# Moving block loads ahead of a write on one DMA queue, and reading partial sums with one DMA instead of four

## The chip, the cores and the metric

The kernel runs on one core of one Trainium2 chip. A core has five engines with an instruction stream each: TensorE (PE), which multiplies matrices and loads their stationary operand (PEld), VectorE (DVE), ScalarE (ACT), GpSimd (POOL) and SyncE (SP), which here only issues DMAs. They synchronise by semaphores. Data move between DRAM and the on-chip memory by 16 DMA engines. The metric is the device time of one execution in microseconds (us); lower is better.

## The reference, cut to what matters

The input is 128 graphs of 128 nodes with 512 features each, and a 0/1 adjacency matrix for each graph. Two layers follow, each with a residual and a layer norm: a graph attention with 8 heads of 64 units, and a hypergraph convolution with a hidden width of 1024.

```python
def _L0_gnn_ref(X, A, W, b, a_self, a_neigh):
    feats = jnp.einsum('bnf,hfu->bhnu', X, W)
    e_self = jnp.einsum('bhnu,hu->bhn', feats, a_self)
    e_neigh = jnp.einsum('bhnu,hu->bhn', feats, a_neigh)
    dense = e_self[..., :, None] + e_neigh[..., None, :]
    dense = jax.nn.leaky_relu(dense, negative_slope=0.2)
    dense = dense + NEG_BIG * (1.0 - A[:, None, :, :])
    att = jax.nn.softmax(dense, axis=-1)
    out = jnp.einsum('bhij,bhju->bhiu', att, feats) + b[None, :, None, :]
    ...
    return jax.nn.relu(out)

def hypergraph_conv(x, adj, W, b):
    H = (adj != 0).astype(x.dtype)
    w = adj.reshape(N, -1)[:, :C]
    xw = jnp.einsum('ncd,hd->nch', x, W)
    Dn = jnp.einsum('nce,ne->nc', H, w)
    Dn = jnp.where(Dn > 0, 1.0 / Dn, 0.0)
    Be = H.sum(axis=1)
    Be = jnp.where(Be > 0, 1.0 / Be, 0.0)
    m = Be[:, :, None] * jnp.einsum('nce,nch->neh', H, xw)
    out = Dn[:, :, None] * jnp.einsum('nce,neh->nch', H, m)
    return out + b
...
h = jax.nn.relu(hypergraph_conv(x, adj, W1, b1))
h = layer_norm(h, gamma, beta)
y = hypergraph_conv(h, adj, W2, b2)
return y + x
...
x = _layernorm(x + _L0_gnn_ref(x, adj, ...), axis=-1)
x = _layernorm(x + _L1_gnn_ref(x, adj, ...), axis=-1)
```

The layer norm of the hidden `h` needs the mean of the squares of `h` over 1024 features for each node.

## The kernel before, in words

The graphs are worked on in 64 pairs. A software pipeline runs over the pairs: in each period of about 36 us one pair is in each of several stages, so that a pair passes from its first load to its store within about five periods. The order of the instructions is written out by hand. Every step has a lag (in periods) and a time (in us, within a nominal period `T = 38.6`); the list `todo` holds all steps of all pairs with the time `(p + lag) * T + time`, is sorted by it, and the instructions are issued in that order. These times are only an order: on the chip each engine goes through its own instructions in this order and waits on semaphores where data or a buffer aren't there yet.

In the text a period begins with the first matmul of `propagate` (output `pz`) of a pair, and a place in it is given in us from there.

The stages that the change and the prediction touch:

- **Loads of a pair.** `load` brings the adjacency (`a`) and its first row, spread over the partitions (`w`); it stands at the very start of the period on SP's queue. `load_blocks` (lines 122 to 129) brings x once more in blocks of 32 nodes, as four DMAs of 128 KB in rows of 512 B, into `xb`. `load_edges` (lines 131 to 137) brings the adjacency in blocks, four DMAs of 32 KB in rows of 128 B, into `ab`. Both tiles have one buffer. They are read by `x_transpose` (line 384, two instructions on DVE, the second at place 35.0 of the written order) and `edges` (line 420, at 35.75), which turn the blocks in place of a transpose on TensorE.
- **Attention scores.** `spread_rows` (line 541) transposes the two score columns of the new features into `rows` on DVE and writes them to DRAM as `rd` (line 551, 16 KB). `neighbours` (line 569) reads `rd` back, spread over all partitions, into `nb`, one DMA of 512 KB for each of the two graphs. POOL adds the mask (line 588), ACT takes the leaky ReLU (line 604), DVE the maximum (line 610) and ACT the exponential (line 618), by half graphs.
- **Turning the exponentials.** `e_write` (line 622) writes the exponentials of a graph to DRAM (`ed`, 512 KB), `e_read` (line 630) reads them back with four DMAs in another order (`eb`), and `e_transpose` (line 639) finishes the transpose on DVE into `eT`. TensorE then multiplies them with the features (`pav`, line 702). SP's queue holds, in this order: `ed` of graph 0, its four `eb`, `ed` of graph 1, its four `eb`. Each `eb` waits on SP until its `ed` has landed, and what stands behind it waits too.
- **Sums of squares.** ACT squares `h` (line 891), POOL adds the squares down to one block of 128 (line 903). `sum_blocks` (lines 949 to 954) transposes and reduces on DVE, `write_sums` (line 959) writes 16 KB to DRAM (`sd`), `read_sums` (line 965) reads 8 rows of 32 numbers with each of four DMAs into `sums_out`, and `sum_rest` (lines 973 and 975) transposes this 128x32 tile on DVE and adds eight numbers for each of the two graphs. The result, after POOL's power (line 1002), scales the output (line 1006).
- **Hidden layer.** `propagate` (line 815, `pz`), its eviction `zT` on ACT (line 828), POOL's sums `zS` (line 839), then the products `ph`, whose matmuls all stand in the helper at line 97. TensorE runs the hidden products, the features (`pf`), the attention (`pav`) and the output products (`py`, `pq`) one after another in a fixed order.

On SP's queue a period so holds: the four reads of sums, `a` and two `w`, `ed` and four `eb`, `ed` and four `eb`, a small write `dd_d` (line 373), four `xb`, the store of a finished pair (line 1041), four `ab`, `rd`, two `nb`, a read `dnb` (line 575), `sd`, and the rows of x for the residual (line 120).

The places of the two block loads in the written order:

```python
for p in range(PAIRS):
    if p > 1:
        todo.append(({2: 79.5, 3: 143.1}.get(p, p * T), load, (p,)))
        todo.append((16.2 if p == 2 else p * T + 19.0, load_blocks, (p,)))
        todo.append((p * T + (28.5 if p == 2 else 20.5), load_edges, (p,)))
```

Of the kernel before, what the change touches and what calls it, by code (L numbers as in the profile page):

```python
# [8 lines left out]
F32 = mybir.dt.float32  # L9
AF = mybir.ActivationFunctionType  # L10
ALU = mybir.AluOpType
AX = mybir.AxisListType
# [8 lines left out]
def kernel(  # L21
# [45 lines left out]
    nc = tc.nc  # L67
    G, N, F = x.shape
    P = 128
# [10 lines left out]
    B = 32  # L80
    NB = P // B

    const = ctx.enter_context(tc.tile_pool(name="const", bufs=1))
    work = ctx.enter_context(tc.tile_pool(name="work", bufs=1))
# [126 lines left out]
    for i in range(2):  # L211
        t = const.tile([P, 2, H, UW + 1], F32, name=f"ft{i}")
# [1 line left out]
        fts.append(t)  # L214
    dn = const.tile([P, B], F32, name="dn")
    nc.gpsimd.memset(dn, 0.0)
    sums_in, sums_out = (const.tile([P, B], F32, name=n) for n in ("sums_in", "sums_out"))
    for t in (sums_in, sums_out):
        nc.gpsimd.memset(t, 0.0)

# [94 lines left out]
    def step(lag, time, since=0, until=PAIRS):  # L315

        def keep(fn):
            steps.append((lag, time, fn.__name__, range(since, until), fn, ()))
            return fn
        return keep  # L320
# [640 lines left out]
    @step(3, 31.5, until=LAST - 1)  # L961
    def read_sums(p, s):

        for c in range(NB):
            nc.sync.dma_start(
                sums_out[c * B:c * B + 2 * NB],
                s["sd"][:, 2 * c:2 * c + 2, :].rearrange("b g n -> b (g n)"),
            )

    @step(4, 1.7, until=LAST - 1)  # L970
    def sum_rest(p, s):
        t = work.tile([P, B], F32, tag="so", name=f"so_{p}")
        nc.vector.transpose(t, sums_out)
        s["ve"] = small.tile([P, 2], F32, tag="ve", name=f"veh_{p}")
        nc.vector.tensor_reduce(
            s["ve"], t[:, :2 * NB].rearrange("p (b g) -> p g b", g=2), AX.X, ALU.add
        )

    @step(3, 43.0, since=LAST - 1, until=LAST)
# [142 lines left out]
    for t, fn, *args in (  # L1122
# [14 lines left out]
    T = 38.6  # L1137
    todo = [
        (11.1, prepare_first, (0,)), (12.0, prepare_first, (1,)), (15.45, prepare_first_sums, ()),
        (12.1, load_weights, (nc.scalar, w2_blocks, w2t, DH // 2, QU)),  # L1140
        (13.05, prepare_vectors, ()),
        (14.05, load_weights, (nc.scalar, w1_blocks[:2], w1t, F // 2, HALF)),
        (12.95, load_first_row, (1,)),
        (15.46, load_weights, (nc.sync, w1_blocks[:1:-1], w1t, F // 2, HALF)),
        (16.1, everywhere, (b2_bc, b2, nc.sync)),
        (79.0, prepare_hidden, (nc.gpsimd, 0)), (79.1, prepare_hidden, (nc.gpsimd, 1)),
# [55 lines left out]
    for p in range(PAIRS):  # L1202
        if p > 1:
            todo.append(({2: 79.5, 3: 143.1}.get(p, p * T), load, (p,)))
            todo.append((16.2 if p == 2 else p * T + 19.0, load_blocks, (p,)))
            todo.append((p * T + (28.5 if p == 2 else 20.5), load_edges, (p,)))
        for lag, time, name, pairs, fn, args in steps:
            if p not in pairs:
                continue
            if p == 0 and lag == 2 and time < 8.5:  # L1210
                time *= 0.2
            if p == LAST:

                time = {
                    ("attend", 0): 24.25, ("attended", 0): 25.5,
                    ("attend", 1): 25.95, ("attended", 1): 26.0,
                    ("residual", 1): 26.3, ("rstds", "a"): 26.4,
                }.get((name,) + args[:1], time)
            if p == LAST - 1:
                time = {  # L1220
                    ("product", 2): 24.22 if (lag, time) > (3, 20.0) else time,
                    ("product", 5): 29.5 if (lag, time) > (3, 20.0) else time,
                    ("squares", 0): 26.5, ("squares", 1): 26.6, ("h_sums", 2): 22.3,
                    ("h_rstd",): 4.6, ("y_scale", 1): 5.8, ("y_scale", 0): 5.9,
                }.get((name,) + args[:1], time)
            time += (p + lag) * T
            todo.append((
                first.get((name, p) + args, first.get((name, p), time)), run, (fn, p, args)
            ))
# [46 lines left out]
```

## Time and profile before

| | |
|---|---|
| time, median of 3 runs | 2395.53 us (2391.52 to 2398.6) |
| the profiled execution | 2395.0 us |
| its span, first to last instruction | 2393.2 us |
| granted TensorE clock, mean | 0.998 of full speed |
| DVE idle before line 973, waiting for `sums_out` | 49.0 us in 36 of 62 times |
| POOL idle before line 588, waiting for `nb` | 30.4 us in 25 times, the longest 5.1 us |
| SP's wait for `ed` to land, before `eb` (line 630) | 375.8 us in 126 times, the longest 5.2 us |
| SP's wait for `sd` to land, before the reads of sums (line 965) | 125.0 us in 62 times |

The profile is that of one execution. Its times belong to that execution and are set against its own 2395.0 us, which lies 1.8 us above its span. "Busy" of an engine is time in an instruction; matmuls are pipelined and their ends are modelled, so a busy TensorE isn't one at its peak. The chain of waits is followed back from the last instruction to what released it at each step. Idle time of an engine that isn't the one others wait for costs nothing. DMA issues on SP show the time that SP takes to issue, not the transfer; the trace also has records of the single packets of the DMA engines, with their start, length and queue, but not which of the 16 engines ran them.

### The profile page before, as it was taken

To read this page: it belongs to the slowest core of one execution; us is meant where nothing else is said; L and a number is where in the kernel's file an instruction comes from. 1 tells how busy PE (TensorE), PEld (TensorE's weight loads), DVE (VectorE), ACT (ScalarE), POOL (GpSimd) and SP (SyncE) were. 2 spreads that over 40 slices of the span, in tenths; PEclk is the share of its full clock that TensorE was granted. 3 is DMA by queue.
4 is the path that set the end of the run, shared out by engine and by line. 5 is a ranking of instruction groups with operands and counts; after the bars stand their busy time and mean duration, and the time that the engine had idled before them with its cause. 6 is when DMAs were issued, how large, how long until landed. Compare 5 with 4: busy or idle time off the path is not lost.

```text
span 2393.2 us, 81039 instructions
## 1 busy us (share of the span) xinstructions
PE 2359.4 (99%) x32309; PEld 1986.4 (83%) x32309; DVE 2079.3 (87%) x4456; ACT 1529.5 (64%) x4481; POOL 1827.5 (76%) x2060
## 2 busy tenths in 40 slices
PE   7999999999999999999999999999999999999998
PEld 6788888888888888888888888888888888888886
DVE  7988888888898898888888888988988988988875
ACT  4565765756667667667667666676676676676663
POOL 5877787777777877877877778778778778777774
PEclk9999999999999999999999999999999999999999
DMA  6545555555455455454554554545554555545541
GB/s 197 133 142 155 142 142 143 146 149 150 139 156 143 144 156 147 140 152 149 146 150 147 149 150 143 156 146 139 155 148 143 153 146 141 151 147 151 148 130 37
DMA packets 432874, 347.12 MB, mean 145 GB/s; under 512 B 153177, under 2 KB 382065, under 8 KB 432497
## 3 DMA queue, kind: packets, MB, share of 16 engines
q1 hardware_dynamic: 429024, 337.46, 49.2%
q8 instruction: 256, 4.19, 0.7%
q10 hardware_dynamic: 3472, 4.47, 0.6%
q14 instruction: 122, 0.99, 0.2%
HBM read 239.08 MB, written 102.73 MB: 143 GB/s over the span
## 4 chain that ended last, share of the span: by engine, by line
PE 81%; DMA 7%; DVE 5%; ACT 2%; POOL 2%; SPq 2%; issue 1%; DVEq 0%; POOLq 0%; ACTq 0%
PE phX L97 16%; PE pyX L97 15%; PE pfX L97 8%; PE phW L97 8%; PE pyW L97 7%; PE phY L97 4%; PE pq L97 4%; PE pfW L97 4%; PE pav L702 4%; PE pz L97 4%; PE pyY L97 4%; DMA nb<-rd 3%; PE pfY L97 2%; DMA rd<-rows 1%; DMA ed<-nb 1%; ACT nb L604 1%
## 5 line engine op out<-in xcount | busy, mean ns | idle before, releaser
L343 ACT COPY py<-pyX 128x257 f32<-128x257 f32 x189 | 70.8, 374 | 533.8 <-PE pyX L97 458.4
L97 PEld LDWEIGHTS phX<-zS,w_sb 128*64 128x64 f32 x6144 | 348.8, 137 | 37.9 <-POOL ft L741 22.3
L97 PE MATMUL phX<-zS,w_sb 128*64 128x128 f32 x6144 | 371.9, 273 | 3.2 <-ACT ph L343 2.9
L903 POOL TENSOR_TENSOR sq<-sq 128x512 f32<-128x512 f32 (+2 forms) x384 | 344.7, 898 | 20.1
L588 POOL TENSOR_TENSOR nb<-nb,neg 128x512 f32<-128x512 f32 x256 | 320.2, 1286 | 31.1 <-DMA nb<-rd 30.4
L604 ACT ACTIVATE nb<-nb,ft 128x128 f32<-128x128 f32 x1020 | 325.1, 392 | 19.4 <-POOL nb L588 19.4
L618 ACT ACTIVATE nb<-nb,nm 128x128 f32<-128x128 f32 x1024 | 319.5, 392 | 5.1 <-DVE nm L610 4.9
L766 POOL TENSOR_TENSOR rso<-veo,mhalf 128x2 f32<-128x2 f32 x63 | 44.2, 702 | 337.6 <-DVE veo L764 337.6
L97 PE MATMUL pyX<-w_sb,h 128*64 128x257 f32 x2016 | 242.8, 379 | 0.5 <-ACT py L343 0.5
L97 PE MATMUL pyX<-w_sb,hS 128*64 128x257 f32 x2016 | 243.1, 379 | 0.0
L97 PE MATMUL pyW<-w_sb,hS 128*64 128x256 f32 x2016 | 242.5, 378 | 0.0
L880 ACT ACTIVATE h<-h,vecs 128x128 f32<-128x128 f32 x768 | 239.9, 394 | 2.5 <-DVE h L865 1.4
L610 DVE TENSOR_REDUCE nm<-nb 128x4 f32<-128x512 f32 x256 | 175.3, 685 | 48.1 <-ACT nb L604 42.7
L97 PEld LDWEIGHTS pyX<-w_sb,h 128*64 128x64 f32 x2016 | 166.4, 136 | 53.5 <-ACT py L343 0.9
L97 PEld LDWEIGHTS pyW<-w_sb,hS 128*64 128x64 f32 x2016 | 168.1, 136 | 50.1 <-issue 0.3
L741 POOL TENSOR_TENSOR ft<-ft,b_bc 128x512 f32<-128x512 f32 x128 | 202.9, 1605 | 6.2 <-ACT ft L532 6.2
L97 PEld LDWEIGHTS pyX<-w_sb,hS 128*64 128x64 f32 x2016 | 161.9, 136 | 43.8
L639 DVE STREAM_TRANSPOSE eT<-eb 128x512 f32<-128x512 f32 x252 | 163.5, 685 | 1.3 <-issue 0.4
L804 DVE SCALAR_TENSOR_TENSOR o<-y,b_bc 128x512 f32<-128x512 f32 x128 | 164.0, 1320 | 0.0
L1006 DVE SCALAR_TENSOR_TENSOR y<-y,rsh,bw_bc 128x512 f32<-128x512 f32 x126 | 150.1, 1229 | 15.2 <-POOL rsh L1002 15.2
L891 ACT ACTIVATE sq<-h 128x512 f32<-128x512 f32 x256 | 160.9, 630 | 2.1
L468 POOL TENSOR_TENSOR hS<-h 128x512 f32<-128x512 f32 x126 | 162.1, 1286 | 0.0
(178 smaller groups left out, 5630.3 us busy)
## 6 DMA issues: line engine op xcount, KB each, us to landing
nb<-rd SPq DMA_DIRECT2D x127, 512.0 KB
ed<-nb SPq DMA_DIRECT2D x126, 512.0 KB
eb<-ed SPq DMA_DIRECT2D x504, 128.0 KB
x<-in_x_dram SPq DMA_DIRECT2D x64, 512.0 KB
out_dram<-o SPq DMA_DIRECT2D x63, 512.0 KB
xb<-in_x_dram SPq DMA_DIRECT2D x248, 128.0 KB
a<-in_adj_dram SPq DMA_DIRECT2D x64, 128.0 KB
w<-in_adj_dram SPq DMA_DIRECT2D x128, 64.0 KB
```

What stands on the lines that cost most here:

```text
L97: nc.tensor.matmul(to[rows], lhs[:, rows], rhs, start=start, stop=stop, skip_group_check=True)
L468: engine.tensor_tensor(t[:, i], in0, in1, op=op)
L588: nc.gpsimd.tensor_tensor(t, t, neg[:, :, None, :].to_broadcast([P, NB, HH, B]), op=ALU.add)
L604: nc.scalar.activation(t, t, AF.Prelu, bias=s["ft"][:, g, h, 0:1], alpha=SLOPE)
L610: nc.vector.tensor_reduce(s["nm"][:, g, hs], scores(p, s, g, hs).rearrange("p b h j -> p h b j"), AX.XY, ALU.max, negate=True,)
L618: nc.scalar.activation(t, t, AF.Exp, bias=s["nm"][:, g, h:h + 1])
L639: nc.vector.transpose(s["eT"][:, g, hs, :].rearrange("p h (b i) -> p h b i", b=NB), s["eb", g][:, :, hs, :].rearrange("p b h j -> p h b j"),)
L741: nc.gpsimd.tensor_tensor(t, t, b0_bc.rearrange("p (h u) -> p h u", h=H), op=ALU.add)
L804: nc.vector.scalar_tensor_tensor(s["o"][:, g, :], s["y"][:, g, :], 2.0, b2_bc, op0=ALU.mult, op1=ALU.add)
L880: nc.scalar.activation(dst[:, k, :], src[:, k, :], AF.Relu, bias=b1_sb[:, c:c + 1])
L891: nc.scalar.activation(s["sq"][:, g, q * KH // 2:(q + 1) * KH // 2, :], hid(s, g, q), AF.Square, scale=DH ** -0.5,)
L903: nc.gpsimd.tensor_tensor(t[:, :n, :], t[:, :n, :], t[:, n:2 * n, :], op=ALU.add)
```

## The change

Two things are changed.

For the pairs from the fifth on (`p` of 4 and more), `load_blocks` moves from 19.0 to 2.0 and `load_edges` from 20.5 to 3.0 in the pair's first period. On SP's queue the eight DMAs so stand behind the loads of `a` and `w` of the same pair and ahead of the first `ed` write of the pair two places before, where they stood behind the second graph's `eb` reads and `dd_d`, the `ab` loads also behind the store. The pairs 2 and 3 keep their places. The order on the other engines stays as it was.

`read_sums` becomes one DMA for four: it reads the whole 4x8x32 numbers as 16 pieces of 64 numbers into partitions 0, 32, 64 and 96 of a `sums_out` that is now 128x256. `sum_rest` transposes all of it (128x256 in place of 128x32), into a work tile of the same size, and adds the first column of each 32x32 block. `sums_out` is set to zero once at the start, as before.

```diff
-    sums_in, sums_out = (const.tile([P, B], F32, name=n) for n in ("sums_in", "sums_out"))
+    sums_in = const.tile([P, B], F32, name="sums_in")
+    sums_out = const.tile([P, NB, 2 * B], F32, name="sums_out")
     for t in (sums_in, sums_out):
         nc.gpsimd.memset(t, 0.0)
...
     @step(3, 31.5, until=LAST - 1)
     def read_sums(p, s):
 
-        for c in range(NB):
-            nc.sync.dma_start(
-                sums_out[c * B:c * B + 2 * NB],
-                s["sd"][:, 2 * c:2 * c + 2, :].rearrange("b g n -> b (g n)"),
-            )
+        nc.sync.dma_start(
+            sums_out[::B],
+            s["sd"][:, :2 * NB, :].rearrange("b (c g) n -> c b (g n)", c=NB),
+        )
 
     @step(4, 1.7, until=LAST - 1)
     def sum_rest(p, s):
-        t = work.tile([P, B], F32, tag="so", name=f"so_{p}")
-        nc.vector.transpose(t, sums_out)
+        t = work.tile([P, NB, 2, B], F32, tag="so", name=f"so_{p}")
+        nc.vector.transpose(t.rearrange("p b g n -> p (b g n)"), sums_out.rearrange("p b x -> p (b x)"))
         s["ve"] = small.tile([P, 2], F32, tag="ve", name=f"veh_{p}")
         nc.vector.tensor_reduce(
-            s["ve"], t[:, :2 * NB].rearrange("p (b g) -> p g b", g=2), AX.X, ALU.add
+            s["ve"], t[:, :, :, 0].rearrange("p b g -> p g b"), AX.X, ALU.add
         )
...
-            todo.append((16.2 if p == 2 else p * T + 19.0, load_blocks, (p,)))
-            todo.append((p * T + (28.5 if p == 2 else 20.5), load_edges, (p,)))
+            todo.append((16.2 if p == 2 else p * T + (19.0 if p == 3 else 2.0), load_blocks, (p,)))
+            todo.append((p * T + {2: 28.5, 3: 20.5}.get(p, 3.0), load_edges, (p,)))
```

## The prediction

> **What bounds the kernel now.** I read the page's busy shares first, then busy time by stretches, the chain of waits, and the issues on SyncE's queue (SP).
>
> ```profile
> PE 2359.4 (99%) x32309; PEld 1986.4 (83%) x32309; DVE 2079.3 (87%) x4456; ACT 1529.5 (64%) x4481; POOL 1827.5 (76%) x2060
> ...
> q8 instruction: 256, 4.19, 0.7%
> ```
>
> TensorE (PE) is busy for 99% of the span, so the question is where its few idle microseconds lie. Two stretches, cut where a period begins (at the first matmul of `propagate`), with the busy time of each engine:
>
> ```profile
> 127.60:645.78 518.18, 512.60 (x7058) 430.10 (x7056) 449.54 (x965) 334.93 (x985) 399.44 (x450) 1.00 0.51 146
> 645.78:2246.14 1600.36, 1600.36 (x22179) 1356.64 (x22177) 1414.90 (x3039) 1048.49 (x3081) 1250.22 (x1409) 1.00 0.52 148
> ```
>
> The second is 44 periods of 36.37 us with PE busy throughout: nothing off PE can shorten them, only lengthen them. The first is 14 periods of 37.01 us on average, an excess of 518.18 - 14 x 36.37 = 9.0 us. That is nearly all the change can win. What it consists of, in the chain that ended last (start, duration):
>
> ```profile
> 596.32 3.42 DMA rd<-rows
> ...
> 599.76 7.18 DMA nb<-rd
> ...
> 611.55 1.97 PE phX L97 x32
> ```
>
> The small write of the neighbour scores to DRAM (`rd`, 16 KB) lands 3.42 us after its issue, only then is the broadcast read `nb` issued, POOL's masking waits 3.0 us for it, then leaky, the eviction of pz, and PE. SP's wait for that landing in the two stretches (total, times, longest):
>
> ```profile
> SPq L569 <- DMA rd<-rows: 35.3, 14, 3.1
> ...
> SPq L569 <- DMA rd<-rows: 48.8, 44, 2.1
> ```
>
> 2.5 us each against 1.1. SP's issues in a period without a stall (start, duration, number):
>
> ```profile
> 645.58 1.88 SPq L965 DMA_DIRECT2D sums_out<-sd  x3
> ...
> 652.40 0.33 SPq L622 DMA_DIRECT2D ed<-nb  x1
> ...
> 663.16 3.18 SPq L129 DMA_DIRECT2D xb<-in_x_dram  x4
> 667.86 0.41 SPq L1041 DMA_DIRECT2D out_dram<-o  x1
> 668.31 2.42 SPq L137 DMA_DIRECT2D ab<-in_adj_dram  x4
> 670.91 0.34 SPq L551 DMA_DIRECT2D rd<-rows  x1
> ```
>
> Here `rd` goes when its data are ready (670.88); in stalled periods the `ab` issues end up to 0.4 us after that. The packet records show what happens then. Of `rd`'s 128 packets 120 run 0.84 to 1.1 us after its issue, stalled or not. In the stalled periods the last eight, one DMA engine's share, come 2.0 to 2.6 us after it, when a 16,384-byte packet of the instruction queue has ended. Such a packet began 0.56 to 0.86 us after the issue of `rd` in six late cases, 1.28 to 1.42 in five, 1.31 in the period before them. From 1.41 on `rd` mostly won, between 1.23 and 1.4 either. So `rd` races an instruction refill; from the page one takes 0.007 x 16 x 2393.2 / 256 = 1.05 us.
>
> **What the Trainium skill says.** "DMA: Bandwidth & Descriptors", Queues, rings and completion order: each DMA engine takes descriptors in ring order and turns between the queue rows it has work for. The eight late packets agree. "Runtime: NRT & Kernel Launch", Instruction fetch mechanics: instructions are refilled in 16 KiB blocks, a cost called mostly hidden. The size agrees (4.19 MB / 256); hidden it is not where `rd` waits. "Perfetto Trace Analysis", DMA Instruction, HWDGE: the profiled window is descriptor generation, not data. This agrees (0.34 us for `rd`, 3.42 to its landing), so issues are priced twice below, on SP and in the rings. "VectorE: DVE Perf Modes", The three transpose paths: 32x32 blocks are transposed each by itself, so one filled row per block becomes the one filled column that `sum_rest` then reads; no run so far shows that layout.
>
> **The change, part by part.** The sum starts from the profiled execution: 2395.0 us, of which 2393.2 are the span; the runs' median, 2395.53, lies 0.5 above.
>
> *Loads moved up.* Per pair from the fifth on, eight issues (four `xb`, 1.9 us; four `ab`, 2.4) pass `ed` and `eb` of both graphs and `dd_d` on SP; `ab` passes the store too. POOL's and the other engines' queues keep their order. The loads wait for the second transpose of x and the edge transpose of the pair before, which end 1.3 us before a period begins: no block for SP.
> (a) `rd` goes at once when `rows` are done and finds the rings emptier. Its first packets came 0.84 us after issue where `ab` had ended early and 0.9 to 0.95 where just before, so it gains 0.1 us there and 0 to 0.4 us on SP. The 9.0 us by the `rd` before each stall: four late ones with the refill at 1.3 to 1.42, or SP late by 0.4 us, cost 3.35; now clear of it, I take 2.9 back. Two (1.28, 1.37), with little gain on SP, cost 2.5: even chances and a smaller loss, 1.6 back. Six (0.56 to 0.86) still meet the refill and cost 3.2: their `nb` goes 0.1 to 0.4 us sooner, and as loss grew from 0.1 to 1 us over a delay of half a microsecond, 1.4 back. Together -5.9; bounds 0 and -9.0. Late next is PE itself.
> (b) In the period at 2246.14 SP reached `rd` 1.35 us late and the next lasts 36.76, 0.39 too much: -0.3, bounds 0 and -0.4.
> (c) The first `ed` write is what gets delayed. Where sums are read early (the period shown), the new order reaches it at 644.9 + 0.65 + 0.5 + 1.0 + 1.9 + 2.4 = 651.4, before its exponentials end at 652.3: no delay. Where late (0.92 us into the period at 1154.92), at 7.4 us instead of 6.6: 0.8 us. In the rings `xb` and `ab` are 1,024 x 27 ns / 16 + 1,024 x 12 ns / 16 = 2.5 us of work, of which I guess up to 1.5 still ahead of `ed`. Behind `ed` on SP stand its `eb` read, the second `ed` and its `eb`, so they move by 0 to 2.3 us. The last `eb` landed 18.3 to 20.5 us into the period where the records tell it; VectorE (DVE), busy without a gap from 9.4 us on, takes it (`eT`) at 22.65 and comes no earlier, and PE needs the result 0.2 to 0.35 us after it is done. Cover 2.2 to 4.3 us: cost 0; if it's gone, each us beyond costs a us in each of 59 periods.
> (d) Start: in the period at 87.39 SP stands until 9.2 us for DVE's `dr`; then 4.3 us of loads put the first `ed` at 13.9 instead of 10.0. Part is made up, as `ed` then took 4.9 us to land; I put the last `eb` at 26.6 to 27.6 against `eT` at 26.6: +0.4, bounds 0 and +1.
>
> *One read for four.* Three issues of 0.60 us and their gaps leave SP in each period: 1.9 us, which pays for much of (c). The new DMA, 16 pieces of 256 B, isn't in the trace; I take 0.65 us of issue and a landing like that of the first of the four, bounds 0.5 and 1.2 on SP. DVE's transpose grows from 128x32 to 128x256, which two rows price:
>
> ```profile
> L949 DVE STREAM_TRANSPOSE sq<-sq 128x256 f32<-128x256 f32 x62 | 27.1, 437 | 0.0
> ...
> L973 DVE STREAM_TRANSPOSE so<-sums_out 128x32 f32<-128x32 f32 x62 | 13.0, 209 | 49.4 <-DMA sums_out<-sd 49.0
> ```
>
> 437 - 209 = 0.23 us, x62 = 14 us, ahead of DVE's own waits for ACT and POOL (1.47, 0.21 and 0.22 us in the period at 645.78), and 49.0 us of waiting for `sums_out` shrink: 0, bounds 0 and +14. The reduction's strided reads, 0 to 0.1 us each, have the same cover; the larger memset stands before POOL's 3.46 us wait for the first weights.
>
> Sum: 2395.0 - 5.9 - 0.3 + 0.4 = 2389.2 us.
>
> **Rivals.** *No change (0.18).* `rd` keeps meeting refills, as both keep their places. For it: six of twelve late cases, and one with `rd` on time (25.13 us in the period at 571.19). Against it: the others were late on SP. It gives 2392 to 2396, say 2394 us.
> *All stalls gone (0.14).* Without the first late ones the lag never starts: 2395.0 - 9.0 - 0.4 = 2385.6 us. Against it: the six early refills.
> *Slower (0.18).* Behind the block loads and a refill (one begins about 9 us into a period), the last `eb` lands after DVE comes for it, and PE waits before the attention matmuls. For it: the loads fill most DMA engines just then. Against it: (c), and stalled periods that issued that `eb` 3 us later without a wait there. It decides from 2.2 to 4.3 us of delay; 0.4 us beyond, 59 x 0.4 = 24 us: 2413 us.
>
> **How the numbers follow.** The forecast has 0.50, its own range 2387 to 2392. Within 0.3% (about what a measurement of this kernel can tell from no change) is 2388.3 to 2402.7. Faster: all of the second rival and 0.24 of the forecast's 0.50, as half its range lies at that bound: 0.38. Same: 0.26 + 0.18 = 0.44. Slower 0.18. The range 2385.0 to 2397.0 leaves out the last case.
>
> **What would show it.** Right: fewer periods over 36.37 us after 127.6, each behind an `rd` that met a refill; `rd` issued within 0.05 us of `rows`; the wait for `sums_out` smaller, `so` at 0.44 us; the first `ed` 0 to 1 us later. Wrong: waits of `pav` for `eT` or of `eT` for `eb` in steady periods; early excess near 9 us, or none.

## The result and the profile after

| | before | after |
|---|---|---|
| time, median of 6 runs each on one chip | 2394.76 us | 2414.18 us (2406.28 to 2414.9) |
| ratio of the runs, with 95% interval | | 1.0076 [1.006, 1.0092] |
| the profiled execution, its span | 2395.0, 2393.2 us | 2406.28, 2404.5 us |

The change makes the kernel slower, by 0.76%. (A ratio here is taken over all runs, not from the medians.) The profiled execution is the quickest of the six runs of after; it carries 11.3 us of the loss. No trace shows where the other 8 us of a usual run lie.

The first line of the page of after, and busy time by stretches of after, cut at the same matmuls as before; the last two rows are 34 and 10 periods (stretch, its length, then busy time of PE, PEld, DVE, ACT and POOL):

```profile
PE 2360.5 (98%) x32309; PEld 2009.4 (84%) x32309; DVE 2083.8 (87%) x4456; ACT 1527.8 (64%) x4481; POOL 1822.8 (76%) x2060
```

```profile
128.73:649.32 520.59, 512.30 (x7058) 435.23 (x7056) 447.21 (x965) 333.13 (x982) 396.47 (x449) 1.00 0.52 145
649.32:1886.21 1236.89, 1236.89 (x17139) 1059.47 (x17136) 1099.43 (x2348) 810.30 (x2382) 966.02 (x1090) 1.00 0.53 148
1886.21:2256.76 370.55, 364.56 (x5042) 312.80 (x5040) 322.21 (x690) 237.72 (x701) 282.69 (x320) 1.00 0.53 145
```

PE's own work is what it was. In the middle stretch it is still back to back, 36.38 us for each period. The loss lies around it. The 14 early periods are 2.4 us longer than before (520.59 against 518.18), although the `rd` stalls should have gone. The ten late ones are 370.55 - 10 x 36.37 = 6.9 us too long, where before their excess was 0.3 us. What lies ahead of the early ones took 1.1 us more; the middle and the end make up the remaining 1.2 us of the 11.3.

The waits of PE, of DVE and of SP in after (who waits, for what: total, times, longest; most lines of after stand one further down than in before):

```profile
PE pav L703 <- DVE eT L640: 13.4, 9, 2.3
```

```profile
DVE eT L640 <- DMA eb<-ed: 17.4, 12, 2.4
```

```profile
SPq L631 <- DMA ed<-nb: 402.3, 126, 5.7
...
SPq L137 <- DMA w<-in_adj_dram: 52.0, 60, 1.6
...
SPq L623 <- DMA xb<-in_x_dram: 23.1, 27, 1.8
```

The attention matmuls wait for the transposed exponentials, these for the last `eb`, and this is what the prediction named as the sign of being wrong. The wait for `sums_out` (49.0 us before) is down to 0.8 us, as forecast. New on SP are two waits that I hadn't priced: 60 times, in 48 periods, the last issues of `ab` stand still until a load of `w` has landed, and in 27 periods the first `ed` (line 623) until an `xb` has. In the periods looked at, the DMA waited for is the one eight places before on SP's queue: the fourth `ab` waits for the second `w`, and `ed` for the first `xb`.

The second worst of the late periods begins at 2182.15. SP's issues in it (start, length, number), and then the chain that ends at its late attention matmul (start, duration):

```profile
2183.56 0.94 SPq L112 DMA_DIRECT2D w<-in_adj_dram  x2
2184.60 2.37 SPq L129 DMA_DIRECT2D xb<-in_x_dram  x4
2187.07 2.88 SPq L137 DMA_DIRECT2D ab<-in_adj_dram  x4
2191.56 0.34 SPq L623 DMA_DIRECT2D ed<-nb  x1
2196.17 1.73 SPq L631 DMA_DIRECT2D eb<-ed  x4
```

```profile
2184.60 6.89 DMA xb<-in_x_dram
...
2191.56 4.59 DMA ed<-nb
...
2198.01 3.48 DMA ed<-nb
...
2202.85 3.79 DMA eb<-ed
...
2206.77 1.32 DVE eT L640 x2
...
2208.22 0.30 PE pav L703 x3
```

The first `xb`, 128 KB, takes 6.89 us to land. `ed` goes at 9.41 us into the period, where 6.62 is usual, and takes 4.59 us to land, since its packets come behind those of `xb` and `ab` and meet an instruction refill. The issue of the last `eb` ends at 21.1 us instead of about 17.4, DVE waits 1.9 us for it, and PE 1.7.

The other half of the change did what it says. The transpose of the sums, from the trace of after (min/median/max ns):

```profile
L973 DVE STREAM_TRANSPOSE so<-sums_out x62: 402/434/446, 96.1 to 2333.2; 128x256 f32<-128x256 f32 x62
```

### The profile page after: what moved, and what is told of

It reads as the page before. It is cut to its first block, busy times and chain, and to the rows that moved or that the text cites. A ratio compares the mean times of both kernels' runs of the same rounds, so it can differ in the third digit from the quotient of the medians.

```text
span 2404.5 us, 80548 instructions
## 1 busy us (share of the span) xinstructions
PE 2360.5 (98%) x32309; PEld 2009.4 (84%) x32309; DVE 2083.8 (87%) x4456; ACT 1527.8 (64%) x4481; POOL 1822.8 (76%) x2060
## 4 chain that ended last, share of the span: by engine, by line
PE 84%; DMA 7%; DVE 5%; SPq 1%; POOL 1%; ACT 1%; issue 1%; DVEq 0%; POOLq 0%; ACTq 0%
PE pyX L97 16%; PE phX L97 15%; PE pyW L97 8%; PE pfX L97 7%; PE phW L97 7%; PE pav L703 5%; PE pz L97 4%; PE pyY L97 4%; PE phY L97 4%; PE pfW L97 4%; PE pq L97 4%; DMA ed<-nb 3%; PE pfY L97 2%; DMA eb<-ed 1%; DMA xb<-in_x_dram 1%; SPq L631 1%
## 5 line engine op out<-in xcount | busy, mean ns | idle before, releaser
L97 PEld LDWEIGHTS phX<-zS,w_sb 128*64 128x64 f32 x6144 | 350.2, 137 | 36.5 <-POOL ft L742 23.1
L589 POOL TENSOR_TENSOR nb<-nb,neg 128x512 f32<-128x512 f32 x256 | 319.7, 1282 | 21.7 <-DMA nb<-rd 21.1
L640 DVE STREAM_TRANSPOSE eT<-eb 128x512 f32<-128x512 f32 x252 | 163.6, 686 | 18.0 <-DMA eb<-ed 17.4
```

The costliest lines, as they stand in the source:

```text
L97: nc.tensor.matmul(to[rows], lhs[:, rows], rhs, start=start, stop=stop, skip_group_check=True)
L589: nc.gpsimd.tensor_tensor(t, t, neg[:, :, None, :].to_broadcast([P, NB, HH, B]), op=ALU.add)
L640: nc.vector.transpose(s["eT"][:, g, hs, :].rearrange("p h (b i) -> p h b i", b=NB), s["eb", g][:, :, hs, :].rearrange("p b h j -> p h b j"),)
```

## The experiments

My theory at first was "lanes": SP's issues are held by the landing of DMAs eight places earlier. The rival "rings" said that the packets of the block loads stand ahead of `ed` in the DMA engines whatever SP waits for. A third blamed the single read. Each ratio is against the kernel before, run beside it on the same chip. The chips differ: on the four that were used, the median of before was 2391.5, 2394.2, 2391.4 and 2391.6 us.

### The two halves, and the halves of the first half

**Loads alone** (`e1_loads_only`): the two lines of the loads' places changed, `read_sums` and `sum_rest` as before.

> Only the loads move up; the sums are still read by four DMAs. My theory (lanes): an issue on SP is held until the DMA eight places before it on SP's queue has landed, so the last two ab issues wait for the slow first-row loads w and ed waits for the first xb; each us of that beyond DVE's cover comes out at TensorE. It expects 2414 to 2430 us, more than the change as a whole, because the 1.9 us that the single read saves SP are missing ahead of ed; SP's waits of ab for w near 52 us in 60 times, waits of pav for eT over 13 us. Rival one (rings): the block loads' packets stand ahead of ed in the DMA engines, whatever SP waits for; it expects about 2414 us as well. Rival two (sums): the single read of sums or the larger transpose on DVE costs the time; it expects 2390 to 2397 us here.

Measured: 2459.9 us, 1.0285 [1.0271, 1.0299], far above every theory. PE's wait in its trace:

```profile
PE pav L702 <- DVE eT L639: 50.3, 29, 2.7
```

The four reads of sums hold SP 1.9 us longer ahead of `ed`. The issue of the last `eb` ends at 20.4 us into a median period, and 32 of the 58 periods from the fourth to the last but three are too long, against 12 in after. So the delay has a threshold: the change as a whole mostly stays below it, this kernel in more than half of its periods not.

**Single read alone** (`e2_one_read`): the loads in their old places.

> Only the read of the sums by one DMA; the loads stay in their old places. Lanes and rings both expect 2390 to 2396 us: SP is 1.9 us freer where it was not short, no wait of ab for w, no wait of pav for eT in steady periods. The rival that blames the single read or the larger transpose expects 2408 us or more.

Measured: 2390.36 us, 0.9995 [0.9986, 1.0003]. The third theory falls. Alone the read moves nothing that can be told apart from no change; with the loads ahead of `ed` it is worth (2459.9 - 2391.5) - (2414.2 - 2394.8) = 49 us, each taken against before on its own chip.

**Edges early, blocks not** (`e3_edges_only`):

```diff
-            todo.append((16.2 if p == 2 else p * T + (19.0 if p == 3 else 2.0), load_blocks, (p,)))
+            todo.append((16.2 if p == 2 else p * T + 19.0, load_blocks, (p,)))
```

> The single read, and of the loads only the four of ab moved up; xb stays behind the second graph's eb and dd_d. Lanes: eight places before the four ab stand DMAs of the pair before that landed long ago, so no ab issue waits for w, ed goes at 6.6 us into the period as before, rd is still clear of the ab issues: 2386 to 2393 us, SP's wait of ab for w below 5 us. Rings: a fifth of the moved bytes (128 of 640 KB) still stands ahead of ed, so a part of the loss stays: 2396 to 2402 us, waits of eT for eb of some us.

Measured: 2388.87 us, 0.9988 [0.9981, 0.9994]: faster than both kernels. `ab` no longer stands ahead of `rd`, and `ed` is not late: 6.62 us in the median period. Four `ab` more in front of it cost nothing.

**Blocks early, edges not** (`e5_blocks_only`):

```diff
-            todo.append((p * T + {2: 28.5, 3: 20.5}.get(p, 3.0), load_edges, (p,)))
+            todo.append((p * T + (28.5 if p == 2 else 20.5), load_edges, (p,)))
```

> The single read, and of the loads only the four of xb moved up; ab stays in its old place. With the 1.9 us of issue of xb set off by the 1.9 us that the single read saves, SP reaches ed as early as before, and eight places before xb stand DMAs that have landed, so no issue waits for w. Rings (now my theory: what stands in the DMA engines ahead of ed delays its landing, and a wait of SP for w is only one form of that): the 512 KB of xb lie ahead of ed, ed lands 0.5 to 1 us later after its issue than in the run with the edges alone, the last eb is issued at 18 to 19.5 us and the time is 2393 to 2404 us. Lanes: nothing waits, 2385 to 2391 us.

Measured: 2399.26 us, 1.0023 [1.0014, 1.0032], as rings said, and not lanes. SP issues `ed` on time (6.62 us in the median), but the wait for its landing grows. From the waits of the run with the single read alone, then of this one:

```profile
SPq L631 <- DMA ed<-nb: 353.2, 126, 4.4
```

```profile
SPq L631 <- DMA ed<-nb: 430.2, 126, 6.2
```

### SP's time or the DMA engines

**Loads ahead of `a` and `w`** (`e4_before_w`):

```diff
-            todo.append((16.2 if p == 2 else p * T + (19.0 if p == 3 else 2.0), load_blocks, (p,)))
-            todo.append((p * T + {2: 28.5, 3: 20.5}.get(p, 3.0), load_edges, (p,)))
+            todo.append((16.2 if p == 2 else p * T + (19.0 if p == 3 else -0.2), load_blocks, (p,)))
+            todo.append((p * T + {2: 28.5, 3: 20.5}.get(p, -0.1), load_edges, (p,)))
```

> The change, but with the eight block loads ahead of a and w in SP's queue instead of behind them. The same DMAs stand ahead of ed and the same bytes; only the order differs, so that eight places before ab stand DMAs that have landed, and eight before ed stands xb's first as in the change. Lanes: no wait of ab for w, ed issued near 6.6 us, waits of pav for eT below 3 us in all, 2387 to 2396 us, unless w now lands after DVE's use of it at 13.9 us, which would show as a wait of w<-a,w for w. Rings: the same bytes ahead of ed, 2408 to 2416 us.

Measured: 2409.62 us, 1.0068 [1.0055, 1.0082]. Lanes as the whole story falls: SP's wait for `w` has gone and `ed` is issued at 6.63 us, but it lands later.

```profile
SPq L631 <- DMA ed<-nb: 471.9, 126, 5.8
```

The second `ed` follows the first after 6.7 us in the median, against 5.6 in after and 5.5 before. What SP no longer waits for, the DMA engines wait for.

**Issues without bytes** (`e9_small`): the loads in their old places, and in their new place eight small DMAs.

```diff
+    def load_small(p):
+        for n in range(8):
+            nc.sync.dma_start(probe[:, n, :], adj[2 * p, 8 * n:8 * n + B, :8])
...
+            if p > 3:
+                todo.append((p * T + 2.0, load_small, (p,)))
```

> Issues without bytes: the single read, the block loads in their old places, and where the change puts them eight small DMAs (32 pieces of 32 B each) into a tile that nothing reads. They do no part of the computation. SP has the eight issues and the same waits for w and for the first of the eight ahead of ed, but the DMA engines have 8 KB there and not 640 KB. If SP's time ahead of ed makes the loss: 2408 to 2416 us, ed issued near 7.0 us in the median. If the bytes ahead of ed make it: 2388 to 2395 us. My theory has both, as ed's issue and its landing add up along one chain: 2394 to 2404 us.

Measured: 2395.13 us, 1.0017 [1.0009, 1.0025]. Eight issues with next to no bytes cost 0.22% against the single read alone (1.0017 - 0.9995), `xb` moved alone 0.28% (1.0023 - 0.9995); the whole change, with `ab`'s bytes too, 0.81%. That is 0.31% over the sum of the two, with an uncertainty of about 0.2% by the four intervals, and the small DMAs bring only a part of SP's waits: 24.3 us for `w` and 3.4 us of `ed` for the first of the eight, where after has 52.0 and 23.1. So the two runs don't split the loss into SP's share and that of the rings.

**Loads behind the first `ed`** (`e7_behind_ed`; `e8_behind_ed_four` is the same with four reads of sums): places 6.3 and 6.4.

> The change, with the eight block loads one step further on: behind ed of graph 0 and ahead of its eb, where SP waits some 5 us for ed to land anyway. rd is as free of them as in the change. Rings and SP both expect the loss to go, since nothing new stands ahead of ed and the 4.3 us of issues lie in a wait: 2384 to 2391 us, the last eb issued near 17 us. A theory in which the moved bytes cost wherever they meet the exponentials' round trip expects more than 2400 us.

> As the run before, with the loads behind ed of graph 0, but with the sums read by four DMAs as in the kernel before. The moved loads then owe nothing to the SP time that the single read saves: 2386 to 2392 us if the place ahead of ed was all that was wrong; 2400 us or more if the loads in the first half of the period need that saving (as the run with the loads alone, 2459.9 us, needed it).

Measured: 2427.35 us, 1.012 [1.0093, 1.0146], and 2418.84 us, 1.0113 [1.0095, 1.0131]: a clear miss. (The runs of the first scatter from 2413 to 2432 us; the two kernels can't be told apart.) SP's issues in a period of the first that begins at 1313.21:

```profile
1319.82 0.33 SPq L623 DMA_DIRECT2D ed<-nb  x1
1320.25 2.27 SPq L129 DMA_DIRECT2D xb<-in_x_dram  x4
1322.62 2.96 SPq L137 DMA_DIRECT2D ab<-in_adj_dram  x4
1325.62 1.88 SPq L631 DMA_DIRECT2D eb<-ed  x4
```

I had taken SP's longest wait for `ed` (5 us) for its usual one. The mean is 353.2 / 126 = 2.8 us, and the eight issues last 5.3. So `eb` goes at 12.4 us into the period, not at 9.2 as in the same period of the run with the single read alone. It is SP's time again, in another place.

**Only `xb` behind `ed`, `ab` ahead** (`e11_blocks_behind`): places 6.3 and 3.0.

> The single read, the four ab ahead of ed of graph 0 as in the run with the edges alone, the four xb behind it, ahead of its eb. With all eight loads there SP needed 5.4 us for the issues (one ab waited for w) where ed had landed 2 to 3.5 us after its issue, so eb came 3 us late. With xb alone the issues take 1.9 us and fit into that wait. If SP's time was the cause there, and the bytes behind ed are harmless: 2385 to 2392 us, eb at most 0.5 us later than in the run with the edges alone. If 512 KB beside ed and eb cost as much as ahead of them: 2396 to 2410 us.

Measured: 2390.34 us, 0.9994 [0.9986, 1.0003]. The 512 KB do no harm there, although the issue of the last `eb` ends at 18.5 us in the median period; in the 58 periods PE never waits for the attention's exponentials. (The `ab` issue of 1.5 us that I put down to `w` in this expectation can't have been that: `w` had landed before.)

**`a` and `w` ahead of the sums** (`e6_rows_early`, the change otherwise): `load` at `p * T - 7.3`.

> The change, with a and w issued ahead of the read of the sums, while SP waits for sd, instead of behind it. The block loads keep their place right ahead of ed. It takes 1.4 us of issue from the stretch ahead of ed and lets w land before the last ab is issued. If what counts is when the block loads get into the rings, their packets are through about 1.4 us sooner and most of the loss goes: 2388 to 2398 us, last eb issued at 17 to 18 us. If the bytes right ahead of ed count whenever they come, it stays at 2405 to 2415 us.

Measured: 2394.33 us, 0.9999 [0.9991, 1.0007]. The loss goes, with the block loads where the change put them. Either the 1.4 us of issues counted, or `w` itself; this run doesn't tell.

**Edges early, and `a` and `w` ahead of the sums from the sixth pair on** (`e10_edges_rows`).

> The edges alone moved up with the single read, and from the sixth pair on a and w issued ahead of the read of the sums too, while SP waits for sd. 1.4 us less of issue ahead of ed where the sums are read late. In the run with the edges alone only 2.8 us of excess were left in the periods 3 to 60, so there is little to gain: 2385 to 2390 us, against 2388.9 of that run; over 2392 us if the sums, now behind w in the rings, come late for DVE.

Measured: 2388.6 us, 0.9989 [0.9983, 0.9996], the same as with the edges alone. There is nothing left to gain at this place.

### What holds the block loads

The packet records of after, in the period at 1886.21, say where `xb` is. It is issued from 2.25 to 4.1 us, and up to 5 us the engines have little to do (packets of 512 B that start in half a microsecond, and the time of all packets that start then, as a share of the 16 engines):

| us into the period | 2.0 | 2.5 | 3.0 | 3.5 | 4.0 | 4.5 | 5.0 | 5.5 | 6.0 |
|---|---|---|---|---|---|---|---|---|---|
| after: packets | 205 | 58 | 40 | 45 | 29 | 64 | 115 | 112 | 222 |
| after: busy | 0.72 | 0.21 | 0.14 | 0.16 | 0.13 | 0.25 | 0.41 | 0.39 | 0.84 |
| plain `w`: packets | 152 | 125 | 151 | 248 | 91 | 13 | 131 | 228 | 165 |
| plain `w`: busy | 0.55 | 0.64 | 0.52 | 0.86 | 0.37 | 0.08 | 0.47 | 0.80 | 0.96 |

(The pause of plain `w` at 4.5 us is an `xb` issue that lasted 1.6 us on SP.) The 205 are mostly `a`; the 40 to 45 are `w`, one packet in about 12 ns over all engines together, 256 of them. "DMA: Bandwidth & Descriptors" in the Trainium skill, Queues, rings and completion order, says that each engine consumes its descriptors in ring order. That would put `xb` behind `w` in every ring and explain engines that are idle with 512 KB queued; the records don't name the engine, so it needs a test. The same slow run of 43 to 46 packets is in the trace of before, from 5.5 to 7.5 us into the period at 1882.47; only `ed` followed it there.

The rows "plain `w`" are those of the run that tests it (`e12_plain_w`), with a control (`e13_one_read_plain_w`) and the order of `e4_before_w` (`e14_before_w_plain`). All three read 128 different rows in place of one row 128 times, so `w` holds the adjacency and not its first row, and the node weights of the result differ:

```diff
-            nc.sync.dma_start(s["w"][:, g, :], adj[2 * p + g, 0, :].partition_broadcast(P))
+            nc.sync.dma_start(s["w"][:, g, :], adj[2 * p + g])
```

> The change, with w loaded as plain rows of the adjacency (the same 128 packets of 512 B for each graph, each from another address) in place of one row read 128 times. The rest is the change: same issues, same bytes, same order. It changes what is computed: w then holds the adjacency and not its first row, so the node weights are wrong. If the slow broadcast w is what holds the block loads and ed (my theory now): w lands in about 2.4 us as a does, SP's wait of ab for w goes from 52 us to below 5, the last eb is issued near 17.5 us in the median and the time is 2388 to 2396 us. If the moved bytes or SP's issues are enough by themselves: 2402 to 2414 us.

> Control: the single read with the loads in their old places, and w loaded as plain rows in the same way; the node weights are wrong here too. Nothing waits for w there, so all theories expect the time of the single read alone, 2387 to 2393 us; if it is faster by more than 3 us, the gain of the run with the change must be read against this one.

> The block loads ahead of a and w (2409.6 us, 1.0068), with w loaded as plain rows; the node weights are wrong here too. If there it was w, right ahead of ed in the DMA engines, that made ed land 1 us later: 2390 to 2397 us and ed's landing back at that of the kernel before. If it was the block loads: 2402 to 2412 us.

Measured: 2391.17 us, 0.9998 [0.9989, 1.0006]; 2389.96 us, 0.9993 [0.9985, 1.0001]; 2392.78 us, 1.0005 [0.9996, 1.0013]. The DMA issues on the pages of after and of the run with the change and plain rows (number, KB, median us to landing):

```profile
xb<-in_x_dram SPq DMA_DIRECT2D x248, 128.0 KB, 5.9
...
w<-in_adj_dram SPq DMA_DIRECT2D x128, 64.0 KB, 5.2
```

```profile
xb<-in_x_dram SPq DMA_DIRECT2D x248, 128.0 KB, 3.2
...
w<-in_adj_dram SPq DMA_DIRECT2D x128, 64.0 KB, 2.1
```

The same bytes, issues and order, with only the addresses of `w` changed, and 0.78% of the time goes (1.0076 - 0.9998), while the same edit is worth 0.02% with the loads in their old places. SP's wait of `ab` for `w` and of `ed` for `xb` are gone, and its wait for `ed` is down, from 402.3 us in after and from 471.9 us with the loads ahead of `w` (the run with the change, then the run with that order, both with plain rows):

```profile
SPq L631 <- DMA ed<-nb: 360.3, 126, 5.1
```

```profile
SPq L631 <- DMA ed<-nb: 353.8, 126, 4.3
```

The slow broadcast is what makes the moved loads dear. It also was what delayed `ed` with the loads ahead of `w`, where it stood directly before `ed`. That much is shown; why one row read 128 times is slow was not tried.

Summary, from the records of each profiled execution, the 58 periods from the fourth to the last but three. The first `ed`, the step to the second `ed` and the end of the last `eb`'s issue are medians; "late" counts the periods in which that issue ends after 19.5 us; excess is the sum over 36.37 us for each period:

| run | ratio | first `ed` issued, us | to the second `ed`, us | last `eb` issued, us | late | excess, us |
|---|---|---|---|---|---|---|
| before | 1 | 6.62 | 5.46 | 17.36 | 9 | 8.8 |
| after | 1.0076 | 7.04 | 5.64 | 18.23 | 12 | 18.5 |
| loads alone | 1.0285 | 8.44 | 5.94 | 20.41 | 34 | 68.8 |
| single read alone | 0.9995 | 6.62 | 5.27 | 17.14 | 0 | 2.9 |
| edges early | 0.9988 | 6.62 | 5.44 | 17.26 | 0 | 2.8 |
| blocks early | 1.0023 | 6.62 | 5.78 | 18.05 | 8 | 10.3 |
| loads ahead of `a`, `w` | 1.0068 | 6.63 | 6.68 | 19.10 | 21 | 18.5 |
| small DMAs | 1.0017 | 6.62 | 5.26 | 17.49 | 3 | 6.1 |
| loads behind `ed` | 1.012 | 6.62 | 7.78 | 19.93 | 53 | 43.6 |
| `xb` behind `ed`, `ab` ahead | 0.9994 | 6.62 | 6.06 | 18.55 | 0 | 2.5 |
| change, plain `w` | 0.9998 | 6.62 | 5.41 | 17.52 | 3 | 5.0 |

The excess follows the late periods and not the median. In after 18.2 of its 18.5 us lie in the 12 late ones; with `xb` behind `ed` the median is later than in after, but no period passes 19.5 us and nothing is lost. Eight of before's 9 late periods are early ones behind a late `rd`; only two of them have a wait of `pav`.

## Why the prediction was wrong, point by point

**The bound** was right: PE, back to back in the steady periods, so that only late inputs can lengthen them.

**(c), the delay of the first `ed`, is the step that failed**, in two of its terms and in its cover. "In the rings `xb` and `ab` are [...] 2.5 us of work, of which I guess up to 1.5 still ahead of `ed`" took the rings to be free. They were held by `w` until about 5 us into the period shown, and `xb` landed 5.9 us after its issue (median). The 1.9 and 2.4 us of loads on SP took the issues to run one after another, and "no block for SP" had only the two buffers in view; the waits eight places back add 52.0 us for `w` in 48 periods, 1.1 us in each, and 23.1 us for `xb` in 27. And the cover of 2.2 to 4.3 us was set against a delay of 0 to 2.3 us, where the last `eb` of the period at 2182.15 comes 3.7 us late (21.1 for 17.4). The first `ed` then goes 0.4 us later in the median, as said, but 8.9 us into the period or later in a tenth of them, and those few pay. A cost of 0 became most of the 19 us: with `w` as plain rows they are gone.

**(a), the gain at `rd`.** The mechanism held: in after `rd` is issued 0.03 us after `rows` each time, a refill that begins 1.21 us or more after it no longer makes it late, and those at 0.62 to 1.07 still do. The size of 5.9 us was too large, and its base of 9.0 us was in good part one execution's: with the single read alone, where `ab` still stands ahead of `rd`, the excess of the profiled execution is 2.9 us. The best versions gain 0.0012 x 2391.5 = 2.9 us on before, and the change with plain `w` nothing that can be told (0.9998, its longer start included): (a) was mis-sized apart from the loss. In after the `rd` that still lose make the next period's inputs late, and that period then stalls at `pav` (2.35 us in the period at 312.73, 2.08 in that at 390.75).

**(b)** was too small to be seen. **(d), the start**, had the right place and too small a size: the periods at 86.96 and 128.73 are 1.6 and 0.6 us longer than before, 2.2 in place of 0.4, beyond its bound of 1. `w` isn't what makes the first of them long: with plain rows it lasts from 86.50 to 128.73.

**The single read** was right in its own terms: 0.434 us for the transpose against 0.44, 0.55 us of issue against 0.65, nothing gained or lost alone. That its 1.9 us "pays for much of (c)" was truer than priced: without it the loads cost 2.85%.

**The rivals.** "Slower" came true at 2414.18 us for 2413, with the waits that it named. The agreement of the numbers is chance: it reckoned 0.4 us in each of 59 periods, and the trace has nine `pav` waits of up to 2.3 us, and carries only 11.3 us of the loss. It laid the delay on the loads themselves and a refill; `w`, in front of them, was in neither its case nor the forecast's. The trace of before did show `w`'s slow packets, and I left them unpriced since nothing waited for them.

## What to carry to other kernels

Before you move a DMA up a queue, look in the packet records at what stands ahead of it there: a slow load can hold what is behind it in the rings even while the engines are nearly idle, and in this program an issue can stand still for a landing eight places back. A load whose slowness costs nothing today can become the bottleneck of whatever is put behind it. And price a delay against the cover of the latest tenth of the periods, not of a median one. Delays on one chain need not add up: the four reads of sums cost nothing that can be told with the loads in their old places, and about 49 us with the loads ahead of `ed`.

## What the runs showed of the hardware that was not expected

- A load of 64 KB that reads one 512-byte row for all 128 partitions lands after 4.2 to 5.2 us (medians of the runs); the same load from 128 different rows lands after 1.9 to 2.1 us.
- In after, an instruction refill stays out of the way of a 16 KB write (`rd`) when it begins 1.21 us or more after the write's issue; one that begins 0.62 to 1.07 us after it holds back the last eight of its 128 packets. In before, with the `ab` loads issued right ahead, refills up to 1.42 us after it did so too. "Runtime: NRT & Kernel Launch" in the Trainium skill, Instruction fetch mechanics, calls the cost of refills mostly hidden; here the late write was waited for.
- An issue on SP can itself last 1.5 to 1.7 us in place of 0.45 (an `ab` with the loads behind `ed`, an `xb` with plain `w`), with no wait recorded. What held it was not looked into.
